# Edge values and queries of a graph layer computed with channels in partitions, then transposed back

## The chip, the cores and the metric

One core of a Trainium2 chip runs the whole kernel. The metric is the device time of one execution in microseconds; the time of a version is the median of its runs. A profiled execution leaves a trace, and all rows quoted here come from it. The engines are called as the profile calls them: PE (TensorE; its weight loads are PEld), DVE (VectorE), ACT (ScalarE), POOL (GpSimd), SP (SyncE, which here only issues DMAs).

## What is computed

A graph attention layer over 6250 nodes and 206250 edges, 64 channels in 4 heads, with a residual and a layer norm. The edge list comes sorted by destination.

```python
Qh = (x @ Wq.T + bq).reshape(n, H, D)
Kh = (x @ Wk.T + bk).reshape(n, H, D)
Vh = (x @ Wv.T + bv).reshape(n, H, D)
Ee = (edge_attr @ We.T + be).reshape(-1, H, D)
score = (Kh[src] * Qh[dst] * (1.0 / np.sqrt(D)) * Ee).sum(-1)
score = jnp.exp(jnp.clip(score, -5.0, 5.0))
msg = Vh[src] * score[..., None]
wV = jax.ops.segment_sum(msg, dst, num_segments=n)
...
x = _layernorm(x + wV.reshape(n, H * D))
```

## The kernel before

**Tiles, groups, steps, rounds.** Edges are cut into 1612 tiles of 128. Eight tiles make a group (202 groups, index g), two groups make a step (s; the last eight groups are steps of their own). Four groups make what is called a round below, and g % 4 (i in the code) is the place in the round: place 0 to place 3. A first stage computes the key and value rows of all nodes into a table in DRAM (`kv_tab`), and the queries of all nodes, split into three bf16 parts, into another. The main loop then runs over g.

**What one group needs.** Keys and values of the source nodes come by indirect DMAs, one a tile, issued by POOL (`gather_kv`, L446) into one of five step buffers; POOL has to wait until the messages of the step that used the buffer are made. Two of the 16 tiles of a step are not gathered but picked: DVE makes one-hot blocks (`hots`, L503), PE multiplies them with the node features (`picks`, L514 and L519, 50 blocks in a round, spread over its four places), ACT copies the result out (`picked`, L526 and L527), PE applies the key and value weights (`picked_kv`, L530 to L535, places 0 and 2), and ACT copies them to the step buffer (`place_kv`, L541, places 1 and 3). The one-hot blocks stand in seven buffers, so a `hots` late in the loop waits for a `picks` two or three pieces back.

**Scores.** `edges` (L560, with the matmuls in L435) multiplies the edge features with the edge weights: the feature block of two tiles (64 channels of each stand in the 128 partitions) is the stationary operand, the block-diagonal weights `we_sb` the moving one of 128 columns. The product stands with edges in partitions and is added onto a bias that ACT has written into that PSUM bank before (`biases`, L564). `queries` (L594) selects the destination's query with a one-hot matrix (`to`, made by ACT in L571 and L577) as the stationary operand of each of the eight tiles. `products` on DVE multiplies the keys with the queries (L600) and the result with the edge values (L601), sums over a head (L604) and clips (L606). `weigh` on ACT is the exponential (L610), `message` on DVE multiplies the values with it (L617).

**Sums.** `onehot_edges` (L585, DVE) and `widen` (L625, ACT) make the one-hot matrix of a step's destinations, `sums` (L630, PE, 16 fp32 matmuls, odd places) adds the messages of its edges, `add` (L644, DVE, even places) adds the sums to a window of node rows. `sums`, `picked_kv`, `place_kv` and `add` use one PSUM bank, `room`.

**Order.** Nothing reorders the work: each engine runs its instructions in the order in which the loop writes them, and waits on semaphores where an operand comes from elsewhere. In iteration g PE runs `picks`, `edges(g+1)`, `sums`, `queries(g+2)`, `picked_kv` (at place 0 the picks come last); ACT the one-hot rows, `widen`, `place_kv`, `biases(g+2)`, `weigh(g)`; DVE `products(g)`, the first `hots`, `add`, `message(g-1)`, `onehot_edges`, the other `hots`. POOL's gathers of the next steps stand behind the message in even iterations. The edge values and the queries have two PSUM banks each.

Of the kernel before, what the change touches and what calls it, by code (L numbers as in the profile page):

```python
# [107 lines left out]
def tile_gnn(ctx: ExitStack, tc: tile.TileContext, x, xT, wT, bias, beT, weT, eT, src, src_rows, dst,  # L108
# [46 lines left out]
    key_rows = consts.tile([NR2, 2, G * P], BF16, name="key_rows")  # L155
# [8 lines left out]
    be_all = consts.tile([P, C], F32, name="be_all")  # L164
# [26 lines left out]
    with tc.tile_pool(name="nodes", bufs=1) as nodes, \  # L191
# [20 lines left out]
        rows_i = nodes.tile([NR2, 2, G * P], I32, name="rows_i")  # L212
        for i in range(NB // CB):
# [15 lines left out]
        nc.sync.dma_start(be_all, beT.to_broadcast([P, C]))  # L229
# [199 lines left out]
    def edge_values(pe, et, n, biased=False):  # L429

        if not biased:
            nc.tensor.matmul(pe[:, :n, :], ones_b, be_p[:, :n, :], start=True, stop=False,
                             skip_group_check=True)
        for u in range(n // 2):
            nc.tensor.matmul(pe[:, 2 * u:2 * u + 2, :], et[:, u, :], we_sb, start=False,  # L435
                             stop=u == n // 2 - 1, skip_group_check=True)
# [20 lines left out]
    with tc.If(rv == 0) as branch:  # L457

        with tc.tile_pool(name="work", bufs=2) as work, \
# [3 lines left out]
            TO, OH, OF, PE, PQ, MSG, KB, SCORE, HOT, FROM, SRC = ({} for _ in range(11))  # L463
# [13 lines left out]
            pe_all = [fixed.tile([P, G, C], F32, name=f"pe{k}") for k in range(2)]  # L477
            pq_all = [fixed.tile([P, G, C], F32, name=f"pq{k}") for k in range(2)]
# [78 lines left out]
            def edges(g):  # L557

                PE[g] = pe_all[g % 2]
                edge_values(PE[g], ET[g], tiles_of(g), g >= 2)  # L560

            def biases(g):
                n = tiles_of(g)
                nc.scalar.activation(pe_all[g % 2][:, :n, :],  # L564
                                     be_all[:, None, :].to_broadcast([P, n, C]), AF.Copy)
# [24 lines left out]
            def queries(g):  # L590
                PQ[g] = pq_all[g % 2]
                n = tiles_of(g)
                for j in range(n):
                    nc.tensor.matmul(PQ[g][:, j, :], TO[g][:, j, :], QW[g], start=j == 0,  # L594
                                     stop=j == n - 1, skip_group_check=True)

            def products(g):
                n = tiles_of(g)
                prod = work.tile([P, G, C], F32, name="prod")
                nc.vector.tensor_mul(prod[:, :n, :], kv_of(g)[:, :n, :C], PQ[g][:, :n, :])  # L600
                nc.vector.tensor_mul(prod[:, :n, :], prod[:, :n, :], PE[g][:, :n, :])  # L601
# [93 lines left out]
            for g in range(4):  # L695
                onehot_rows(g)
                onehot_rows_rest(g)
# [262 lines left out]
```

## Time and profile before

| | |
|---|---|
| median of 3 runs | 2490.64 us (2482.57 to 2494.39) |
| profiled execution | 2496.53 us, of it 2494.6 us between its first and last instruction |
| mean granted TensorE clock | 0.825 |
| PE, DVE, ACT, POOL busy | 78%, 60%, 36%, 54% |
| matmul records, weight-load records | 12299, 12299 |

The profile's page counts an engine as busy while an instruction runs on it; matmul ends are modelled, so that the distance between two starts says more than a duration. An fp32 matmul leaves two records, a bf16 matmul and a transpose one. In a row of the timeline the first number is the start, the second the time until the last of the merged instructions ends, and the bracket tells how long the engine stood idle before and which instruction's signal ended it; "remote" and "issue" mean that no instruction of the trace was found to have ended the wait. POOL runs the gathers one behind the other; an unbroken row of them is called a run below.

### The profile page before, as it was taken

The page shows a single profiled execution, that of the slowest core. Times are in us where ns is not written, and L with a number is a line of the kernel's source. Part 1 is how long each engine was busy: PE and PEld are TensorE (multiplying, and loading weights), DVE is VectorE, ACT ScalarE, POOL GpSimd, SP SyncE. Part 2 cuts the span into 40 slices and gives each one's busy share as a digit, 9 for nine tenths or more (in the row PEclk, how much of TensorE's full clock was granted, in tenths as well). Part 3 has the DMA queues.
Part 4 walks back from the last instruction along what each step waited for, and adds up shares of the span by engine and source line. Part 5 has one row for each costly group of instructions (what it writes and reads, how often), then busy time and mean ns, then how long its engine had stood idle before and what let it go on. Part 6 is the DMA issues. An engine that isn't in the chain of part 4 may idle for free. (4 is left out here: it accounts for less than half of the span.)

```text
span 2494.6 us, 32642 instructions
## 1 busy us (share of the span) xinstructions
PE 1935.9 (78%) x12299; PEld 1331.1 (53%) x12299; DVE 1494.2 (60%) x2314; ACT 908.6 (36%) x1268; POOL 1350.8 (54%) x1434
## 2 busy tenths in 40 slices
PE   4477887887887887877778788788788778788875
PEld 4435555555555555455555555555555555455574
DVE  2356665665666666666556566566666666666653
ACT  1242433433442434233424234233343343342452
POOL 5435555555555555555555555555555555555551
PEclk9978888887887888788788788788888788888865
DMA  4332333333332333333323233233333332332341
GB/s 119 125 96 77 100 91 86 99 97 82 99 97 80 98 91 104 87 83 97 95 82 92 79 101 98 78 99 90 91 103 86 88 101 79 95 93 83 87 114 25
DMA packets 140877, 228.84 MB, mean 92 GB/s; under 512 B 71126, under 2 KB 71576, under 8 KB 140598
## 3 DMA queue, kind: packets, MB, share of 16 engines
q1 hardware_dynamic: 94758, 133.30, 18.3%
q0 software_dynamic: 45568, 92.37, 14.2%
q8 instruction: 98, 1.61, 0.3%
q10 hardware_dynamic: 384, 1.00, 0.2%
q14 instruction: 69, 0.57, 0.1%
HBM read 218.74 MB, written 7.79 MB: 91 GB/s over the span
## 5 line engine op out<-in xcount | busy, mean ns | idle before, releaser
L446 POOL DMA_INDIRECT kv<-kv_tab,src_i x1392 | 1319.3, 948 | 1086.1 <-DVE msg L617 642.3
L503 DVE TENSOR_TENSOR hot<-from,still 128x2048 bf16<-128x2048 bf16 (+1 forms) x611 | 697.2, 1173 | 156.9 <-PE low L519 117.0
L630 PE MATMUL room<-msg,off 128*128 128x64 f32 x3224 | 498.3, 298 | 284.8 <-issue 277.4
L630 PEld LDWEIGHTS room<-msg,off 128*128 128x128 f32 x3224 | 472.9, 220 | 304.3 <-issue 296.0
L514 PE MATMUL pick<-hot,parts 128*128 128x512 bf16 x2350 | 583.8, 401 | 9.3 <-issue 9.0
L541 ACT ACTIVATE kv<-room 128x256 f32<-128x256 f32 x94 | 36.2, 385 | 1379.0 <-PE room L630 511.8
L514 PEld LDWEIGHTS <-parts 128*128 128x128 bf16 x2350 | 235.7, 103 | 299.1 <-issue 88.7
L601 DVE TENSOR_TENSOR prod<-prod,pe 128x512 f32<-128x512 f32 x202 | 138.8, 687 | 418.4 <-remote 323.7
L435 PE MATMUL pe<-we_sb,et 128*128 128x128 f32 x1612 | 292.0, 331 | 110.5 <-ACT pe L564 68.9
L435 PEld LDWEIGHTS pe<-we_sb,et 128*128 128x128 f32 x1612 | 243.3, 229 | 182.7 <-ACT pe L564 88.9
L519 PE MATMUL low<-hot,parts 128*64 128x512 bf16 x2350 | 306.1, 386 | 14.5 <-issue 13.8
L577 ACT ACTIVATE to<-to,one_p 126x1024 bf16<-126x1024 bf16 x202 | 232.0, 1148 | 6.6
L571 ACT ACTIVATE to<-kb,minus_row 126x1024 bf16<-126x1024 bf16 x202 | 230.0, 1139 | 10.9 <-remote 5.5
L519 PEld LDWEIGHTS <-parts 128*64 128x64 bf16 x2350 | 120.3, 110 | 190.0 <-issue 114.8
L625 ACT ACTIVATE off<-of 128x2048 f32<-128x2048 bf16 (+2 forms) x105 | 191.9, 1828 | 52.5 <-remote 20.8
L644 DVE SCALAR_TENSOR_TENSOR acc<-room,above,acc 128x64 f32<-128x64 f32 x103 | 29.0, 282 | 243.2 <-ACT kv L541 177.9
L600 DVE TENSOR_TENSOR prod<-kv,pq 128x512 f32<-128x512 f32 x202 | 137.5, 681 | 25.2 <-remote 6.8
L594 PE MATMUL pq<-qw,to 126*128 126x64 bf16 x1612 | 109.7, 217 | 50.4 <-issue 40.2
L617 DVE TENSOR_TENSOR msg<-kv,score 128x512 f32<-128x512 f32 x202 | 138.7, 687 | 16.9 <-ACT score L610 12.7
L604 DVE TENSOR_REDUCE score<-prod 128x32 f32<-128x512 f32 x202 | 138.3, 685 | 6.9
L594 PEld LDWEIGHTS <-to 126*128 126x128 bf16 x1612 | 103.4, 120 | 61.1 <-issue 56.5
L585 DVE TENSOR_TENSOR of<-still,key 128x2048 bf16<-128x2048 bf16 (+2 forms) x105 | 123.3, 1175 | 0.2
(122 smaller groups left out, 1050.1 us busy)
## 6 DMA issues: line engine op xcount, KB each, us to landing
et<-in_eT SPq DMA_DIRECT2D x100, 512.0 KB
kb<-key_tab SPq DMA_DIRECT2D x201, 252.0 KB
kv<-kv_tab,src_i POOLq DMA_INDIRECT x1392
srcs<-in_src_rows SPq DMA_DIRECT2D x47, 256.0 KB
qw<-q_tab SPq DMA_DIRECT2D x202, 15.8 KB
kv_tab<-kv_sb SPq DMA_DIRECT2D x5, 640.0 KB
q_tab<-q SPq DMA_DIRECT2D x5, 480.0 KB
acc<-in_x SPq DMA_DIRECT2D x48, 32.0 KB
```

The source lines that it names most:

```text
L435: nc.tensor.matmul(pe[:, 2 * u:2 * u + 2, :], et[:, u, :], we_sb, start=False, stop=u == n // 2 - 1, skip_group_check=True)
L446: nc.gpsimd.indirect_dma_start(out=kv_of(g)[:, j, :], out_offset=None, in_=kv_tab[:, :], in_offset=bass.IndirectOffsetOnAxis(ap=src_i[:, t ...
L503: nc.vector.tensor_tensor(HOT[m, c][:, :hi - lo].rearrange("p b (a c) -> p b a c", c=2), pairs(FROM[m])[:, None].to_broadcast(shape), bloc ...
L514: nc.tensor.matmul(hi_mid, parts_flat[:, at:at + 2 * C], hot, start=b == 0, stop=b == NB - 1)
L519: nc.tensor.matmul(low[u * C:(u + 1) * C], parts_flat[:, at:at + C], hot, start=b < 2, stop=b >= NB - 2, skip_group_check=True)
L571: nc.scalar.activation(TO[g][:, :n, :], KB.pop(g)[:, :n * P].rearrange("p (j e) -> p j e", j=n), AF.Square, bias=minus_row3[:3 * W])
L577: nc.scalar.activation(TO[g][:, :n, :], TO[g][:, :n, :], AF.Relu, bias=one_p[:3 * W], scale=-1.0)
L594: nc.tensor.matmul(PQ[g][:, j, :], TO[g][:, j, :], QW[g], start=j == 0, stop=j == n - 1, skip_group_check=True)
L601: nc.vector.tensor_mul(prod[:, :n, :], prod[:, :n, :], PE[g][:, :n, :])
L617: nc.vector.tensor_mul(MSG[s][:, k:k + n, :].rearrange("p g (h d) -> p g h d", h=H), kv_of(g)[:, :n, C:].rearrange("p g (h d) -> p g h d", ...
L625: nc.scalar.activation(OF[s][:, :n, :], OH.pop(s)[:, :n, :], AF.Copy)
L630: nc.tensor.matmul(pa, OF[s][:, j, :], MSG[s][:, j, :], start=j == 0, stop=j == n - 1)
```

## The change

The edge values are computed with the weights as the stationary operand and the edge features of eight tiles as 512 moving columns: one fp32 matmul in place of four of 128 columns, its result with channels in partitions and edges in columns. ACT copies it to SBUF and adds the bias in one instruction, since a channel's bias is now one value a partition (`biased`). The queries are made the same way round: the query window is the stationary operand, the one-hot rows of four tiles the 512 moving columns, two bf16 matmuls in place of eight, the second into the other 64 partitions (`queries`). DVE multiplies the two there (`terms`). PE turns the product back by four transposes of 128 by 128 (`turn`), and `products` is left with one multiplication by the keys. In PSUM `ee` and `qq` are single banks, and the turned product has two.

In the loop `edges` runs three groups ahead, `turn` one, `queries` and `terms` two. PE now runs `edges`, `turn`, `queries` before `sums`; `terms` stands at the end of DVE's iteration, behind all `hots`; ACT runs `weigh` ahead of `widen`, `biased` and `place_kv`. Edge features are fetched one block of two groups earlier. `key_rows` moves to a pool that is freed before the main loop, and `prod` has one buffer.

```diff
-    def edge_values(pe, et, n, biased=False):
-
-        if not biased:
-            nc.tensor.matmul(pe[:, :n, :], ones_b, be_p[:, :n, :], start=True, stop=False,
-                             skip_group_check=True)
...
-            pe_all = [fixed.tile([P, G, C], F32, name=f"pe{k}") for k in range(2)]
-            pq_all = [fixed.tile([P, G, C], F32, name=f"pq{k}") for k in range(2)]
+            ee = fixed.tile([P, G // 2, P], F32, name="ee")
+            qq = fixed.tile([P, G // 2, P], F32, name="qq")
+            qe = [fixed.tile([P, G, C], F32, name=f"qe{k}") for k in range(2)]
...
             def edges(g):
 
-                PE[g] = pe_all[g % 2]
-                edge_values(PE[g], ET[g], tiles_of(g), g >= 2)
-
-            def biases(g):
+                n = tiles_of(g) // 2
+                nc.tensor.matmul(ee[:, :n, :], we_sb, ET[g][:, :n, :], start=True, stop=True)
+
+            def biased(g):
+
+                n = tiles_of(g) // 2
+                EB[g] = work.tile([P, G // 2, P], F32, name="eb")
+                nc.scalar.activation(EB[g][:, :n], ee[:, :n], AF.Identity, bias=be_col)
+
+            def queries(g):
+
                 n = tiles_of(g)
-                nc.scalar.activation(pe_all[g % 2][:, :n, :],
-                                     be_all[:, None, :].to_broadcast([P, n, C]), AF.Copy)
+                for u in range(2):
+                    nc.tensor.matmul(qq[u * C:(u + 1) * C, :n // 2, :], QW[g], TO[g][:, u:n:2, :],
+                                     start=True, stop=True)
+
+            def terms(g):
+
+                n = tiles_of(g) // 2
+                TERM[g] = work.tile([P, G // 2, P], F32, name="term")
+                nc.vector.tensor_mul(TERM[g][:, :n], EB.pop(g)[:, :n], qq[:, :n])
+
+            def turn(g):
+
+                for u in range(tiles_of(g) // 2):
+                    nc.tensor.transpose(qe[g % 2][:, 2 * u:2 * u + 2, :].rearrange("p j c -> p (j c)"),
+                                        TERM[g][:, u, :], ident)
...
-            def queries(g):
-                PQ[g] = pq_all[g % 2]
-                n = tiles_of(g)
-                for j in range(n):
-                    nc.tensor.matmul(PQ[g][:, j, :], TO[g][:, j, :], QW[g], start=j == 0,
-                                     stop=j == n - 1, skip_group_check=True)
-
             def products(g):
                 n = tiles_of(g)
-                prod = work.tile([P, G, C], F32, name="prod")
-                nc.vector.tensor_mul(prod[:, :n, :], kv_of(g)[:, :n, :C], PQ[g][:, :n, :])
-                nc.vector.tensor_mul(prod[:, :n, :], prod[:, :n, :], PE[g][:, :n, :])
+                prod = work.tile([P, G, C], F32, name="prod", bufs=1)
+                nc.vector.tensor_mul(prod[:, :n, :], kv_of(g)[:, :n, :C], qe[g % 2][:, :n, :])
...
-                if g % LG == 0 and g + 2 * LG < NG:
-                    fetch_edges(g // LG + 2)
+                if g % LG == 0 and g + 3 * LG < NG:
+                    fetch_edges(g // LG + 3)
...
-                if 2 <= g + 1 < NG:
-                    edges(g + 1)
+                if g + 3 < NG:
+                    edges(g + 3)
+                if i == 0 and 4 <= g <= 4 * LAST + 2:
+                    picked_kv(0)
+                if g + 1 < NG:
+                    turn(g + 1)
+                if g + 2 < NG:
+                    queries(g + 2)
                 if g - 2 in ends:
                     sums(ends[g - 2])
-                if g + 2 < NG:
-                    queries(g + 2)
-                if i in (0, 2) and 4 <= g <= 4 * LAST + 2:
-                    picked_kv(i // 2)
+                if i == 2 and 4 <= g <= 4 * LAST + 2:
+                    picked_kv(1)
...
                 for mc in ahead[1:]:
                     hots(*mc)
+                if g + 2 < NG:
+                    terms(g + 2)
```

**PE, place 3 of the round of g = 96 to 99.** Before, from the last pick on (`pe` are edge values, `pq` queries; `x4` and `x16` are matmuls of which each leaves two records):

```order
L519 LDWEIGHTS parts
L519 MATMUL low<-hot,parts 64x512
L435 MATMUL pe_883<-we_sb,et 128x128 x4
L630 MATMUL room<-msg,off 128x64 x16
L594 LDWEIGHTS to
L594 MATMUL pq_886<-qw,to 128x64
```

Now, from the same pick on, in the changed kernel's own line numbers (`ee` edge values, `qe` the turned product, `qq` queries, L643 `sums`):

```order
L520 LDWEIGHTS parts
L520 MATMUL low<-hot,parts 64x512
L561 MATMUL ee<-et,we_sb 128x512
L585 MATMUL qe_886<-ident,term 128x128 x4
L573 LDWEIGHTS qw
L573 MATMUL qq<-to,qw 64x512
L573 LDWEIGHTS qw
L573 MATMUL qq<-to,qw 64x512
L643 MATMUL room<-msg,off 128x64 x16
```

The queries have moved from behind the sums to ahead of them, and the four transposes stand there too.

**DVE, from the end of place 3 (g = 99) to the message of place 0 (g = 100).** Before, from the last one-hot block of g = 99:

```order
L503 TENSOR_TENSOR hot<-from,still 128x1024
L600 TENSOR_TENSOR prod<-kv_67,pq_885 128x512
L601 TENSOR_TENSOR prod<-prod,pe_883 128x512
L604 TENSOR_REDUCE score<-prod 128x32
L606 TENSOR_SCALAR score<-score 128x32
L503 TENSOR_TENSOR hot<-from,still 128x2048
L644 SCALAR_TENSOR_TENSOR acc<-room,above,acc 128x64
L644 SCALAR_TENSOR_TENSOR acc<-room,below,acc 128x64
L617 TENSOR_TENSOR msg<-kv_71,score 128x512
```

Now, from the same block (L580 is `terms` of g = 101, L614 the one multiplication left in `products` of g = 100):

```order
L504 TENSOR_TENSOR hot<-from,still 128x1024
L580 TENSOR_TENSOR term<-eb,qq 128x512
L614 TENSOR_TENSOR prod<-kv_67,qe_886 128x512
L617 TENSOR_REDUCE score<-prod 128x32
L619 TENSOR_SCALAR score<-score 128x32
L504 TENSOR_TENSOR hot<-from,still 128x2048
L657 SCALAR_TENSOR_TENSOR acc<-room,above,acc 128x64
L657 SCALAR_TENSOR_TENSOR acc<-room,below,acc 128x64
L630 TENSOR_TENSOR msg<-kv_71,score 128x512
```

As many instructions stand there as before. The first multiplication before needed queries that PE had made an iteration earlier, and the second the edge values of place 3; now the first one needs the queries that PE makes in place 3.

More of the change, by code (lines that the diff above doesn't have):

```diff
@@ L154, in tile_gnn @@
     below = consts.tile([P, 7, 32], F32, name="below")
-    key_rows = consts.tile([NR2, 2, G * P], BF16, name="key_rows")
     n_wide = consts.tile([1, 1], I32, name="n_wide")
@@ L163, in tile_gnn @@
     parts_flat = parts.rearrange("p b i c -> p (b i c)")
-    be_all = consts.tile([P, C], F32, name="be_all")
+    be_col = consts.tile([P, 1], F32, name="be_col")
     acc = consts.tile([P, RING, C], F32, name="acc")
@@ L212, in tile_gnn @@
         rows_i = nodes.tile([NR2, 2, G * P], I32, name="rows_i")
+        key_rows = nodes.tile([NR2, 2, G * P], BF16, name="key_rows")
         for i in range(NB // CB):
@@ L228, in tile_gnn @@
         nc.sync.dma_start(be_sb, beT.to_broadcast([3, C]))
-        nc.sync.dma_start(be_all, beT.to_broadcast([P, C]))
+        for i in range(2):
+            nc.sync.dma_start(be_col[i * C:(i + 1) * C, :], beT.rearrange("o c -> c o"))
         nc.vector.memset(we_sb, 0.0)
@@ L427, in tile_gnn, with edge_values @@
                 rest_of_x()
-    def edge_values(pe, et, n, biased=False):
-        if not biased:
-            nc.tensor.matmul(pe[:, :n, :], ones_b, be_p[:, :n, :], start=True, stop=False,
-                             skip_group_check=True)
+    def edge_values(pe, et, n):
+        nc.tensor.matmul(pe[:, :n, :], ones_b, be_p[:, :n, :], start=True, stop=False,
+                         skip_group_check=True)
         for u in range(n // 2):
@@ L462, in tile_gnn @@
                 tc.tile_pool(name="psum", bufs=1, space=bass.MemoryType.PSUM) as psum:
-            TO, OH, OF, PE, PQ, MSG, KB, SCORE, HOT, FROM, SRC = ({} for _ in range(11))
+            TO, OH, OF, EB, TERM, MSG, KB, SCORE, HOT, FROM, SRC = ({} for _ in range(11))
             still = fixed.tile([P, 4 * P], F32, name="still")
@@ L697, in tile_gnn @@
                 onehot_rows_rest(g)
+            fetch_edges(2)
             for g in range(2):
                 edges(g)
+                biased(g)
                 queries(g)
+                terms(g)
+            turn(0)
+            edges(2)
+            biased(2)
             for mc in pieces(0):
@@ L738, in tile_gnn @@
                     onehot_rows_rest(g + 4)
-                if i == 2 and g < 4 * LAST:
-                    sources(m + 1)
-                if g - 1 in ends:
-                    widen(ends[g - 1])
-                if i in (1, 3) and 4 <= g <= 4 * LAST + 3:
-                    place_kv(m - 1, i // 2)
-                if g + 2 < NG:
-                    biases(g + 2)
                 if now:
@@ L750, in tile_gnn @@
                     add(NS - 2)
+                if g - 1 in ends:
+                    widen(ends[g - 1])
+                if g + 3 < NG:
+                    biased(g + 3)
+                if i == 2 and g < 4 * LAST:
+                    sources(m + 1)
+                if i in (1, 3) and 4 <= g <= 4 * LAST + 3:
+                    place_kv(m - 1, i // 2)
                 if before:
```

## The prediction

> **What bounds the kernel now.** First the busy shares and the list of waits (engine and line that waited, what for, total us, times, longest us).
>
> ```profile
> PE 1935.9 (78%) x12299; PEld 1331.1 (53%) x12299; DVE 1494.2 (60%) x2314; ACT 908.6 (36%) x1268; POOL 1350.8 (54%) x1434
> ...
> POOL kv L446 <- DVE msg L617: 642.3, 139, 27.2
> ...
> DVE prod L601 <- remote: 323.7, 41, 9.5
> ...
> PE room L630 <- issue: 277.4, 385, 1.8
> DVE acc L644 <- ACT kv L541: 177.9, 43, 5.3
> ```
>
> No engine is full. PE stands highest, but part of its time is a stall that no operand explains ("issue", in `sums`), and DVE loses 323.7 us before the second multiplication of `products`, 7.9 us at a time. The timeline of one round shows what ties these together. Rows of PE, DVE, ACT and POOL, in order of time:
>
> ```profile
> 1216.49 0.95 POOL L446 DMA_INDIRECT kv<-kv_tab,src_i  x1 [3.69 <-DVE msg L617]
> ...
> 1222.03 1.16 PE L435 MATMUL pe<-we_sb,et 128*128 128x128 f32 x8
> ...
> 1223.03 1.56 PE L630 MATMUL room<-msg,off 128*128 128x64 f32 x13
> ...
> 1232.75 0.94 POOL L446 DMA_INDIRECT kv<-kv_tab,src_i  x1 [0.30 <-issue]
> ...
> 1236.27 1.33 PE L630 MATMUL room<-msg,off 128*128 128x64 f32 x6 [0.91 <-issue]
> ...
> 1236.32 0.69 DVE L601 TENSOR_TENSOR prod<-prod,pe 128x512 f32<-128x512 f32 x1 [8.26 <-remote]
> 1237.04 0.69 DVE L604 TENSOR_REDUCE score<-prod 128x32 f32<-128x512 f32 x1
> ...
> 1237.64 0.39 ACT L541 ACTIVATE kv<-room 128x256 f32<-128x256 f32 x1 [14.64 <-PE room L630]
> 1237.76 0.18 DVE L606 TENSOR_SCALAR score<-score 128x32 f32<-128x32 f32 x1
> 1237.85 1.21 DVE L503 TENSOR_TENSOR hot<-from,still 128x2048 bf16<-128x2048 bf16 x1
> ...
> 1238.98 0.28 DVE L644 SCALAR_TENSOR_TENSOR acc<-room,above,acc 128x64 f32<-128x64 f32 x1
> ...
> 1239.37 0.68 DVE L617 TENSOR_TENSOR msg<-kv,score 128x512 f32<-128x512 f32 x1
> ...
> 1240.32 0.94 POOL L446 DMA_INDIRECT kv<-kv_tab,src_i  x1 [6.62 <-DVE msg L617]
> ...
> 1248.84 1.22 DVE L503 TENSOR_TENSOR hot<-from,still 128x2048 bf16<-128x2048 bf16 x1 [4.20 <-PE low L519]
> ...
> 1250.93 0.95 POOL L446 DMA_INDIRECT kv<-kv_tab,src_i  x1 [3.41 <-DVE msg L617]
> ...
> 1254.09 3.68 PE L630 MATMUL room<-msg,off 128*128 128x64 f32 x32
> 1254.76 0.69 DVE L601 TENSOR_TENSOR prod<-prod,pe 128x512 f32<-128x512 f32 x1
> 1257.61 0.40 PE L594 MATMUL pq<-qw,to 126*128 126x64 bf16 x8
> ...
> 1262.31 0.39 ACT L541 ACTIVATE kv<-room 128x256 f32<-128x256 f32 x1 [15.79 <-remote]
> ...
> 1262.73 0.28 DVE L644 SCALAR_TENSOR_TENSOR acc<-room,above,acc 128x64 f32<-128x64 f32 x1 [5.22 <-ACT kv L541]
> ...
> 1263.36 0.69 DVE L617 TENSOR_TENSOR msg<-kv,score 128x512 f32<-128x512 f32 x1 [0.16 <-ACT score L610]
> ...
> 1264.32 0.95 POOL L446 DMA_INDIRECT kv<-kv_tab,src_i  x1 [3.69 <-DVE msg L617]
> ```
>
> Look at 1223.2: the edge values that DVE needs in L601 are done there (eight records from 1222.03, each 0.125 us, the next work starting at 1223.03), and DVE gets the signal at 1236.32. In place 1 the sums are done by 1257.8, and ACT, which waits for them, starts at 1262.31. PE's signals are held back while POOL's gathers run: a run of 14 (the last at 1232.75) began at 1216.49 and let go 19.8 us later, a run of 8 began at 1250.93 and let go 11.4 us later, a run of 6 began at 1240.32 and the wait for PE ended 8.5 us later. That is 1.42 us a gather each time. Late in the long hold PE itself slows: 13 matmuls in 1.56 us at 1223.03, then waits without a cause, 385 of them in the trace and 0.72 us each. So a round is three holds and three short answers between them: 19.8, then 4.00 (1236.32 to 1240.32), 8.5, then 2.1 (1248.84 to 1250.93), 11.4, then 2.0 (1262.31 to 1264.32), together 47.8, which is 1264.32 less 1216.49. The holds are counted in gathers, and the change leaves all 28 of them. **What the change can alter are the answers**: what DVE and ACT have to do between a signal's release and the message that frees POOL.
>
> **The change part by part.** The costs of single operations, from the groups by line:
>
> ```profile
> L526 ACT ACTIVATE x<-pick 128x512 f32<-128x512 f32 x47 | 27.6, 587 | 0.0
> ...
> L564 ACT ACTIVATE pe<-be_all 128x512 f32<-128x512 f32 x200 | 117.4, 587 | 12.4 <-DVE prod L601 11.2 <-issue 1.2
> ...
> L600 DVE TENSOR_TENSOR prod<-kv,pq 128x512 f32<-128x512 f32 x202 | 137.5, 681 | 25.2 <-remote 6.8 <-issue 6.4 <-PE room L535 3.9
> ```
>
> *ACT and DVE work.* `biased` copies 128x512 from PSUM, as L526 does in 587 ns; `biases`, which goes, took 587. DVE's two multiplications of 681 and 687 ns become two of the same shape, one operand in PSUM each. Neither engine's total changes.
>
> *PE work, by group.* Edge values: eight fp32 records of 128 columns become two of 512, the same number of columns, 1.0 us either way. Queries: eight records took 0.23 us (1257.61 to the next work at 1257.84); two with 512 columns cost between 0.24 and 0.46 us, from the rows below: twelve `low` matmuls, which alternate between the two halves of the partitions, need 1.41 us, 0.24 a pair, and twelve `pick` ones at most 2.76 us, 0.23 each. I take the pair, since the change also writes the two halves. Transposes: not in the main loop before; four fp32 records of 128 columns are bounded below by L435's 0.125 us each, 0.5 together, and above by four times L386's 424 ns, 1.7 us. I take 0.5, nearer to the distance of the prologue's transposes: four from 111.41 to 112.45, 0.26 each, twice L435's, as it would be at half clock.
>
> ```profile
> 111.41 1.12 PE L386 MATMUL tp<-ident,xs 128*128 128x128 f32 x4
> 112.45 1.11 PE L406 MATMUL ps<-ident,xT_sb 64*128 64x64 f32 x8
> ...
> 1257.84 2.76 PE L514 MATMUL pick<-hot,parts 128*128 128x512 bf16 x12
> ...
> 1237.39 0.63 PE L594 MATMUL pq<-qw,to 126*128 126x64 bf16 x8
> 1238.57 2.07 PE L435 MATMUL pe<-we_sb,et 128*128 128x128 f32 x8 [0.54 <-ACT pe L564]
> ...
> 1251.68 1.49 PE L519 MATMUL low<-hot,parts 128*64 128x512 bf16 x12
> 1253.09 1.16 PE L435 MATMUL pe<-we_sb,et 128*128 128x128 f32 x8
> ```
>
> So PE gains about 0.5 us of work a group and loses instructions: 32 records (weight loads counted) become 16. [...]
>
> *What hides the PE work.* In place 1 the sums end at 1257.8 and are held until 1262.3: 4.5 us of cover for 0.5. In place 3 all of it lies under the long hold. In place 2 PE waits for `place_kv` and for fresh one-hot blocks anyway. In place 0 nothing covers it, and at half clock each step costs nearly double (2.07 us for the edge values at 1238.57, 1.16 at 1222.03): 1.0 for the transposes, less 0.63 for the queries of place 3, which are made before the hold now, less the 0.54 of waiting for `biases`, which goes: -0.2, nothing.
>
> *The answer of place 0.* Before the hold, DVE had done L600, and on release it ran L601, L604, L606, one `hots`, two `add` and the message, 4.00 us to POOL's start. Now it stands at `terms`, one multiplication earlier, behind a signal (queries) that PE gives after 16 records from its last pick (2+2 for the edge values, 4+4 for the transposes, 2+2 for the queries), where the edge values needed 16 before. If the signal is held as that one was, the answer grows by one multiplication, **0.69 us, times the 41 waits: +28 us**. `place_kv` at 1237.64 is no later, and DVE's `add` is the last to be ready.
>
> *The answer of place 2.* The message waits for `weigh`, which now runs ahead of `place_kv`; that wait goes. All of it, by the row of L617:
>
> ```profile
> L617 DVE TENSOR_TENSOR msg<-kv,score 128x512 f32<-128x512 f32 x202 | 138.7, 687 | 16.9 <-ACT score L610 12.7 <-issue 3.5 <-ACT pe L564 0.6
> ```
>
> -13 us. The last eight groups, without picks, gain transposes and lose waits for `biases`: nothing.
>
> *Sum.* +28 - 13 = +15 us on the profiled 2496.5 us. The median of the runs shown is 5.9 us lower: 2490.6 + 15 = **2506 us**.
>
> **The rivals.**
>
> *A, the queries get through.* At place 3 the signal may pass before the hold closes, or early in it: in place 1, L601 ran at 1254.76, 3.8 us into a run of 8. Then DVE does `terms`, the products and one `hots` during the hold, and on release only `place_kv`, `add` and the message remain: add at 1238.0 (end of L541) and not 1238.98, -1.0 us; if the sums are through by then too, ACT starts at 1236.3 and it is -2.3 us. Times 41, less 13 us: 2437 to 2383 us. Against it: as many records stand ahead of the signal as before, in the same place of the run, and 41 of the 47 rounds (x47 in L526) show the wait.
>
> *B, slower: the queries of place 1 are caught.* There `terms` needs a signal that PE gives some 0.7 us after the edge values, 4 us into the run of 8. Edge values at 3.2 us passed; sums at 6.8 were held until 11.4. If the hold closes before 4 us, DVE is stopped ahead of `products` and one `hots`, and the answer of 2.0 us grows by 0.69+0.68+0.69+0.18+1.21 less the 0.42 of waiting for ACT: 3.0 us, times 47: 2506 + 141 = 2647. For it speaks the single signal at 3.2; against it, that queries stand ahead of the 64 records of the sums.
>
> *C, nothing comes of it.* DVE's wait of 4.20 us at 1248.84 is for a pick of PE that ends at about the same time as the hold of 8.5 us. If PE sets it, 0.69 us of DVE ahead of it cost nothing: 2490.6 - 13, or with half of the +28, 2478 to 2492.
>
> *D, slower: PE sets the pace.* Transposes at L386's 424 ns add 1.2 us a group to the 0.5; in place 0, uncovered, 1.2 to 2.4 us times 47: 2562 to 2619. [...] The clock column of the windows shows half clock (0.50) after the hold, in which PE was busy 0.44 of 2 us:
>
> ```profile
> 1226.00:1228.00 2.00, 0.44 (x3) 0.30 (x2) 2.00 (x3) 0.00 (x0) 1.39 (x3) 1.00 0.11 33
> 1238.00:1240.00 2.00, 1.46 (x7) 1.43 (x7) 2.00 (x5) 2.00 (x6) 0.00 (x0) 0.50 0.00 0
> ```
>
> **How the numbers follow.** Forecast 0.42, its own range 2478 to 2533 (from none of the 28 us to all of it with the gain of place 2 absent and 0.3 us more of PE's work showing in place 0, 47 times); A 0.28; C 0.12; B 0.10; D 0.08. A change under 0.5% (2478 to 2503) is about what a measurement here cannot tell from none. The forecast's range has about half in that band and half above; A lies below, C within or a little under it, B and D above. Faster 0.31, same 0.29, slower 0.40. The range leaves out the lower part of A and all of B: 2410 to 2600.
>
> **What would show it.** Right: DVE waits about 8 us for PE at `terms` in some 40 rounds, no longer in `products`; from that release to POOL's next gather 4.7 us; the holds still 1.42 us a gather; L617 no longer waits for ACT; ACT's and DVE's busy time as before; PE's `turn` records 0.125 us apart at full clock. A shows as that wait gone or short and the answer at 2 to 3 us; B as a wait at `terms` in place 1 that ends 11.4 us after the run's start; D as DVE waiting for PE outside the holds. Wrong altogether would be a hold that depends on PE's own records: with 16 fewer a group it would shrink, and the round with it, beyond A.

## The result, and the profile after

The changed kernel takes 2428.11 us (median of 4 runs, 2424.42 to 2431.01) beside 2488.17 us for the kernel before (4 runs): ratio 0.9757, 95% interval 0.9729 to 0.9786. Forecast were 2506 us and an answer that grows; it shrank. The busy shares and waits of the changed kernel, in the columns of the prediction's (its `terms` are L580, `products` L614 to L619, `weigh` L623, `message` L630, `sums` L643, `add` L657, `place_kv` L542, `edges` L561, `biased` L567, `queries` L573, `turn` L585):

```profile
PE 1953.4 (81%) x10687; PEld 1157.5 (48%) x10687; DVE 1479.8 (61%) x2314; ACT 931.0 (38%) x1270; POOL 1352.1 (56%) x1434
...
POOL kv L446 <- DVE msg L630: 584.4, 139, 38.5
...
DVE acc L657 <- ACT kv L542: 336.6, 80, 7.4
...
DVE term L580 <- remote: 183.9, 33, 10.0
...
PE room L643 <- issue: 127.1, 165, 1.9
```

POOL waits 58 us less. DVE's wait for a held signal is still there, at `terms`, but 184 us in place of 324. DVE waits longer in `add` instead, 337 us in place of 178: it is through with its other work earlier and stands there until the release. PE's unexplained stalls in `sums` fell from 277 us to 127. The timeline of the changed kernel, two holds and the answers behind them:

```profile
1223.21 0.94 POOL L446 DMA_INDIRECT kv<-kv_tab,src_i  x1 [3.46 <-DVE msg L630]
...
1234.55 0.38 ACT L542 ACTIVATE kv<-room 128x256 f32<-128x256 f32 x1 [8.43 <-PE low L520]
...
1234.78 0.60 PE L585 MATMUL qe<-ident,term 128*128 128x128 f32 x4
...
1234.96 0.28 DVE L657 SCALAR_TENSOR_TENSOR acc<-room,above,acc 128x64 f32<-128x64 f32 x1 [5.34 <-ACT kv L542]
...
1235.36 0.68 DVE L630 TENSOR_TENSOR msg<-kv,score 128x512 f32<-128x512 f32 x1
...
1236.31 0.94 POOL L446 DMA_INDIRECT kv<-kv_tab,src_i  x1 [3.42 <-DVE msg L630]
...
1242.44 0.41 PE L573 MATMUL qq<-to,qw 126*64 126x512 bf16 x2
...
1242.78 3.99 PE L643 MATMUL room<-msg,off 128*128 128x64 f32 x32
...
1244.10 0.69 ACT L567 ACTIVATE eb<-ee,be_col 128x512 f32<-128x512 f32 x1 [1.51 <-PE room L643]
...
1246.86 0.68 DVE L580 TENSOR_TENSOR term<-eb,qq 128x512 f32<-128x512 f32 x1
...
1247.46 0.68 DVE L614 TENSOR_TENSOR prod<-kv,qe 128x512 f32<-128x512 f32 x1
...
1248.99 1.21 DVE L504 TENSOR_TENSOR hot<-from,still 128x2048 bf16<-128x2048 bf16 x1
...
1252.81 0.94 POOL L446 DMA_INDIRECT kv<-kv_tab,src_i  x1 [0.30 <-issue]
...
1256.33 0.38 ACT L542 ACTIVATE kv<-room 128x256 f32<-128x256 f32 x1 [11.54 <-remote]
...
1256.75 0.28 DVE L657 SCALAR_TENSOR_TENSOR acc<-room,above,acc 128x64 f32<-128x64 f32 x1 [6.55 <-ACT kv L542]
...
1257.14 0.68 DVE L630 TENSOR_TENSOR msg<-kv,score 128x512 f32<-128x512 f32 x1
...
1258.09 0.94 POOL L446 DMA_INDIRECT kv<-kv_tab,src_i  x1 [4.34 <-DVE msg L630]
```

The run of 14 starts at 1236.31 and lets go 20.0 us later, at 1256.33, as before. But `terms` ran at 1246.86, in the middle of it and without any wait (the row has no bracket), and with it the products and a block of comparisons. All 32 matmul records of the sums went through in 3.99 us; before, 13 did, and the rest trickled. So only `place_kv`, `add` and the message are left at the release: 1.8 us to POOL's start, where it was 4.00.

This round is not the usual one: in 38 of 48 runs of 14 DVE does wait at `terms`, by more than 0.5 us. A usual round, and one in which the signal is held to the end:

```profile
868.99 0.94 POOL L446 DMA_INDIRECT kv<-kv_tab,src_i  x1 [3.49 <-DVE msg L630]
...
884.60 0.69 DVE L580 TENSOR_TENSOR term<-eb,qq 128x512 f32<-128x512 f32 x1 [4.98 <-remote]
...
890.82 0.94 POOL L446 DMA_INDIRECT kv<-kv_tab,src_i  x1 [4.39 <-DVE msg L630]
...
2152.25 0.94 POOL L446 DMA_INDIRECT kv<-kv_tab,src_i  x1 [3.58 <-DVE msg L630]
...
2172.10 0.69 DVE L580 TENSOR_TENSOR term<-eb,qq 128x512 f32<-128x512 f32 x1 [10.01 <-remote]
...
2176.71 0.94 POOL L446 DMA_INDIRECT kv<-kv_tab,src_i  x1 [7.29 <-DVE msg L630]
```

A `terms` that starts 15.6 us after the run still leaves time for the products before the release, and the next run comes after 21.8 us, as in the first round. One that starts after 19.9 us does not: the answer is then 4.6 us.

From the starts of POOL's runs in both traces (run of 14 to run of 6 to run of 8 to the next run of 14, mean of the rounds that show the pattern):

| us | before | after |
|---|---|---|
| 14 to 6 | 23.93 (33 rounds) | 22.15 (43) |
| 6 to 8 | 10.39 (43) | 10.32 (43) |
| 8 to 14 | 12.95 (33) | 13.17 (43) |
| first run of 8 in the loop | 213.1 | 221.2 |
| span | 2494.6 | 2422.5 |

A round is 1.6 us shorter, 47 times 77 us; 8 us of it are lost at the start. The step that gained is place 0, from the run of 14 to the run of 6. The step from 8 to 14 gained nothing on the mean.

### The profile page after: what moved, and what is told of

Its sections match the earlier page's. It is cut to its first block, busy times and chain, and to the rows that moved or that the text cites. A ratio compares the mean times of both kernels' runs of the same rounds, so it can differ in the third digit from the quotient of the medians.

```text
span 2422.5 us, 29177 instructions
## 1 busy us (share of the span) xinstructions
PE 1953.4 (81%) x10687; PEld 1157.5 (48%) x10687; DVE 1479.8 (61%) x2314; ACT 931.0 (38%) x1270; POOL 1352.1 (56%) x1434
## 4 chain that ended last, share of the span: by engine, by line
PE 61%; another core or an unknown queue 19%; DVE 8%; ACT 6%; issue 6%; DMA 0%; POOL 0%; DVEq 0%; SPq 0%; ACTq 0%; POOLq 0%
PE pick L515 19%; PE room L643 11%; PE low L520 10%; PE ee L561 7%; PE qe L585 4%; DVE hot L504 3%; PE room L534 3%; PE qq L573 3%; PE room L536 2%; ACT to L598 1%; ACT off L638 1%; ACT eb L567 1%; ACT to L592 1%; PE room L531 1%
## 5 line engine op out<-in xcount | busy, mean ns | idle before, releaser
L643 PE MATMUL room<-msg,off 128*128 128x64 f32 x3224 | 440.6, 288 | 133.5 <-issue 127.1
L643 PEld LDWEIGHTS room<-msg,off 128*128 128x128 f32 x3224 | 412.8, 204 | 161.6 <-issue 153.3
L580 DVE TENSOR_TENSOR term<-eb,qq 128x512 f32<-128x512 f32 x202 | 138.2, 684 | 327.2 <-remote 183.9
L561 PE MATMUL ee<-et,we_sb 128*128 128x512 f32 x404 | 268.6, 736 | 80.3 <-issue 50.4
L542 ACT ACTIVATE kv<-room 128x256 f32<-128x256 f32 x94 | 36.0, 383 | 770.4 <-remote 362.2
L567 ACT ACTIVATE eb<-ee,be_col 128x512 f32<-128x512 f32 x202 | 136.3, 675 | 502.7 <-PE ee L561 224.0
L657 DVE SCALAR_TENSOR_TENSOR acc<-room,above,acc 128x64 f32<-128x64 f32 x103 | 29.2, 283 | 374.0 <-ACT kv L542 336.6
L585 PEld LDWEIGHTS qe<-ident,term 128*128 128x128 f32 x806 | 121.7, 166 | 88.7 <-issue 72.1
L531 PE MATMUL room<-bkv_p,ones_b 3*128 3x256 bf16 x94 | 31.4, 334 | 156.3 <-DVE acc L657 152.1
L585 PE MATMUL qe<-ident,term 128*128 128x128 f32 x806 | 147.6, 315 | 4.5 <-DVE term L580 4.5
L561 PEld LDWEIGHTS ee<-et,we_sb 128*128 128x128 f32 x404 | 71.7, 212 | 154.6 <-issue 114.2
L614 DVE TENSOR_TENSOR prod<-kv,qe 128x512 f32<-128x512 f32 x202 | 137.5, 681 | 3.8 <-issue 0.2
```

What stands on the lines that cost most here:

```text
L561: nc.tensor.matmul(ee[:, :n, :], we_sb, ET[g][:, :n, :], start=True, stop=True)
L567: nc.scalar.activation(EB[g][:, :n], ee[:, :n], AF.Identity, bias=be_col)
L585: nc.tensor.transpose(qe[g % 2][:, 2 * u:2 * u + 2, :].rearrange("p j c -> p (j c)"), TERM[g][:, u, :], ident)
L643: nc.tensor.matmul(pa, OF[s][:, j, :], MSG[s][:, j, :], start=j == 0, stop=j == n - 1)
```

## Experiments

The runs landed on different chips, and these are of two kinds. On some the kernel before takes 2488 to 2546 us, with the holds; here called **held**. On the others it takes 1826 to 1831 us and shows no hold; here called **free**. The comparison above is of the held kind. Each ratio is to the kernel before on the same chip. On a held chip the changed kernel itself was measured only in the comparison above, not beside the runs below.

### The order alone, the form alone

before_order: the kernel before in the new order, as far as it goes.

```diff
-                if g - 2 in ends:
-                    sums(ends[g - 2])
+                if i == 0 and 4 <= g <= 4 * LAST + 2:
+                    picked_kv(0)
                 if g + 2 < NG:
                     queries(g + 2)
-                if i in (0, 2) and 4 <= g <= 4 * LAST + 2:
-                    picked_kv(i // 2)
+                if g - 2 in ends:
+                    sums(ends[g - 2])
+                if i == 2 and 4 <= g <= 4 * LAST + 2:
+                    picked_kv(1)
...
+                if now:
+                    weigh(g)
...
                 if g - 1 in ends:
                     widen(ends[g - 1])
```

> The kernel before with the new order alone where that is possible: queries and the first placing matmuls ahead of the sums, the exponential ahead of the widening and the placing; edge values and queries in their old form. Count: the edge values' signal stands behind as many records as before and the sums behind 16 to 34 more, so the 19.8 us hold catches it, DVE waits 8 us in products, 2470 to 2500 us (place 2 gains at most 17 us). Place: most of the gain of the change is there, 2430 to 2460 us.

split_both: the changed kernel with 24 PE records a group more.

```diff
-                nc.tensor.matmul(ee[:, :n, :], we_sb, ET[g][:, :n, :], start=True, stop=True)
+                for u in range(n):
+                    nc.tensor.matmul(ee[:, u, :], we_sb, ET[g][:, u, :], start=u == 0,
+                                     stop=u == n - 1, skip_group_check=True)
...
-                    nc.tensor.matmul(qq[u * C:(u + 1) * C, :n // 2, :], QW[g], TO[g][:, u:n:2, :],
-                                     start=True, stop=True)
+                    for j in range(n // 2):
+                        nc.tensor.matmul(qq[u * C:(u + 1) * C, j, :], QW[g], TO[g][:, 2 * j + u, :],
+                                         start=j == 0, stop=j == n // 2 - 1, skip_group_check=True)
```

> The changed kernel, but edge values made in four matmuls of 128 columns (not one of 512) and queries in eight of 128 columns (not two of 512): same columns, same order, same results, 24 more PE records a group (weight loads counted). Theory 'count' (how much of PE's work gets its signal out during a run of gathers depends on the number of PE records in it): the signal that the multiplication of the terms waits for falls back to the end of the hold in most rounds, 19.8 us after the run of 14 started, DVE waits some 8 us there, and the time goes back to 2480 to 2510 us. Theory 'place' (it is the order: queries ahead of the sums, and the deeper pipeline): DVE gets its signal at 8 to 12 us as in the changed kernel, and the time stays within 15 us of it, 2425 to 2443.

Both landed on a free chip: before_order 1.0022 (1.0012 to 1.0032), split_both 1.0151 (1.0126 to 1.0175). Without a hold they decide nothing. before_order_2 (1.0028), before_order_3 (1.0036) and split_both_2 (1.0184) are the same kernels, again on free chips; then each met a held chip.

> The same kernel as split_both once more, for a chip on which PE's signals are held. Count: 2465 to 2520 us where the kernel before takes 2490. Place: 2420 to 2445. Where the kernel before takes 1828: 1855 to 1862.

> The same kernel as before_order, for a chip on which PE's signals are held (the kernel before at 2490 to 2550 us). Count alone: ratio to the kernel before 0.99 to 1.03. Order worth most of the gain: 0.97 to 0.985. Where the kernel before takes 1828: 1834.

| held chip | us | kernel before there | ratio, 95% |
|---|---|---|---|
| split_both_3 | 2681.40 | 2546.22 | 1.0542 (1.0506 to 1.0578) |
| before_order_4 | 2627.31 | 2542.51 | 1.0325 (1.0298 to 1.0351) |

Both ratios lie beyond what either theory had written, on the side of 'count'. With the records put back, the new form loses more than the whole gain: it has 40 records a group for edge values, turning and queries, where the kernel before has 32. And the new order with the old form is a loss, not a part of the gain. The timeline of split_both_3 in a run of 14 shows how:

```profile
1205.39 0.94 POOL L446 DMA_INDIRECT kv<-kv_tab,src_i  x1 [3.64 <-DVE msg L633]
...
1213.15 0.30 PE L576 MATMUL qq<-to,qw 126*64 126x128 bf16 x2
...
1215.45 0.30 PE L576 MATMUL qq<-to,qw 126*64 126x128 bf16 x2 [0.49 <-issue]
...
1223.96 0.27 PE L646 MATMUL room<-msg,off 128*128 128x64 f32 x1 [0.94 <-issue]
...
1224.66 0.27 PE L646 MATMUL room<-msg,off 128*128 128x64 f32 x1 [0.44 <-issue]
...
1225.37 4.74 PE L646 MATMUL room<-msg,off 128*128 128x64 f32 x21 [0.44 <-issue]
...
1225.58 0.69 DVE L583 TENSOR_TENSOR term<-eb,qq 128x512 f32<-128x512 f32 x1 [9.54 <-remote]
...
1230.15 0.38 ACT L542 ACTIVATE kv<-room 128x256 f32<-128x256 f32 x1 [4.01 <-PE room L646]
...
1231.91 0.94 POOL L446 DMA_INDIRECT kv<-kv_tab,src_i  x1 [9.07 <-DVE msg L633]
```

PE is already slowed in the queries (L576), and then issues one weight load and one matmul of `sums` per 0.70 us. The signal of the queries comes with the release, 20.2 us into the run, and 21 of the 32 matmuls of `sums` are still to be done behind it. The answer is 6.3 us, 1225.58 to 1231.91. In before_order_4 it is the same with 20 matmuls left, and 6.2 us:

```profile
1225.64 0.94 POOL L446 DMA_INDIRECT kv<-kv_tab,src_i  x1 [3.65 <-DVE msg L617]
...
1245.58 4.53 PE L630 MATMUL room<-msg,off 128*128 128x64 f32 x20 [0.43 <-issue]
1245.74 0.69 DVE L601 TENSOR_TENSOR prod<-prod,pe 128x512 f32<-128x512 f32 x1 [8.54 <-remote]
...
1250.15 0.38 ACT L541 ACTIVATE kv<-room 128x256 f32<-128x256 f32 x1 [17.76 <-PE room L630]
...
1251.91 0.94 POOL L446 DMA_INDIRECT kv<-kv_tab,src_i  x1 [9.10 <-DVE msg L617]
```

Counted over the runs of 14 of all held traces (but the one before the loop has settled): the PE records (weight loads and matmuls) from the start of the run to the last matmul that DVE waits for (`edges` in the old form, `queries` in the new), and when DVE's second multiplication after the start of the run began, in us after that start. It is the one that the quoted rounds show waiting.

| kernel | records, median | start, median | later than 19 us |
|---|---|---|---|
| after | 82 | 14.6 | 6 of 48 |
| picked_late | 93 | 19.7 | 29 of 53 |
| both_late | 93 | 18.8 | 24 of 48 |
| before | 97 | 19.9 | 39 of 44 |
| before_order_4 | 99 | 20.1 | 44 of 46 |
| split_both_3 | 132 | 20.2 | 46 of 47 |

Within the changed kernel alone the rounds differ too. With 69 to 75 records DVE does not wait at all and starts at 9.8 to 10.6 us (8 rounds; so do two with 82, at 9.8 and 11.3). Among the rounds with a wait, the start is at 12.1 us with 72 to 79 records (median of 3), 15.3 with 80 to 87 (18) and 17.0 with 88 to 95 (14). That is some 0.25 us a record, with much scatter (12.1 to 19.9 us within 80 to 87 alone), not far from the 0.35 at which a slowed PE goes on (0.70 a pair, above). So within this kernel the signal comes later, in the median, the more records PE has issued since the run began, up to the end of the hold. Why is not shown, and the count is not all: with 88 to 95 records the new form starts at 17.0 us, but the kernel before at 19.8 (19 rounds). What else holds the old form back stays open.

### The placing matmuls of place 0

picked_late, and both_late, which has the start of start_early (below) as well:

```diff
-                if i == 0 and 4 <= g <= 4 * LAST + 2:
-                    picked_kv(0)
                 if g + 1 < NG:
                     turn(g + 1)
                 if g + 2 < NG:
                     queries(g + 2)
+                if i == 0 and 4 <= g <= 4 * LAST + 2:
+                    picked_kv(0)
```

> The changed kernel with the placing matmuls of place 0 behind the turning and the queries, where the kernel before had them, in place of ahead of them. PE waited 58.8 us there in 46 rounds for the two additions of DVE (1.3 us a round), with the turning and the queries queued behind. Theory 'PE's queue' (where no signal is held, PE sets the pace of the changed kernel, and the kernel before with four transposes added was no slower because its PE does not wait there): POOL's 1348 gathers take 1690 to 1702 us, and not 1717, the time is 1832 to 1842 where the kernel before takes 1828. Rival (PE's own work sets it): 1850 to 1858. Where the kernel before takes about 2490: the turning and the queries of place 0 are made during the hold, the hold stays, 2415 to 2430.

> The same edit together with the start of the run start_early. PE's queue: the start was worth 3.5 us while PE set the pace; with PE's wait gone POOL's gathers set it, and the earlier start counts in full, 4 to 8 us off picked_late: 1824 to 1836 where the kernel before takes 1828. Rival (PE's own work sets it): 1846 to 1855. Where the kernel before takes about 2490: 2405 to 2425.

Both met a held chip (before 2490.23 us): picked_late 2464.30 us, 0.9869 (0.9834 to 0.9905); both_late 2462.29 us, 0.9870 (0.9828 to 0.9912). The expected 2405 to 2430 were missed by 35 us: the order that frees PE from a wait puts more records ahead of the signal (93, not 82), the rounds lose their regular 14, 6, 8, and about half of the gain goes. What they would do on a free chip was not seen.

### The change where nothing is held

> The changed kernel as it is, on the chip that this call gets. The kernel before took 2488 us where it was compared with the change, with PE's signals held during runs of gathers, and 1828 us on the chip of the last four runs, where no wait of DVE is put down to 'remote' and POOL's gathers run almost without a break. Theory 'hold' (the gain of 60 us is a shorter answer to the holds and nothing else): where the kernel before takes about 1828 us, the change gains nothing and the PE work that it adds (4 transposes of 0.125 us each a group, at 202 groups, less what queries and the waits for the biases cost) shows, since PE is busy over 90% of the span: 1835 to 1875 us, slower by 0.5 to 2.5%. Where the kernel before takes about 2488, it is 2428 again. Rival 'shorter path' (the change makes the chain itself shorter, by the form or the order): faster than the kernel before by 1 to 3% in either place.

> The kernel before as it is, for its trace on the chip of this call. Hold: if it takes about 1828 us, no DVE wait on 'remote', POOL starts a gather every 1.25 us across the ends of the runs, PE is busy over 90% and its sums show no waits without a cause; if it takes about 2488, the three holds of 19.8, 8.5 and 11.4 us are there.

Free chip: changed kernel 1856.50 us, ratio 1.0155 (1.0132 to 1.0178); kernel before 1827.70. POOL's groups by line, and its start behind the one long wait, for the kernel before:

```profile
PE 1676.6 (92%) x12299; PEld 1148.1 (63%) x12299; DVE 1490.3 (82%) x2314; ACT 907.5 (50%) x1268; POOL 1363.0 (75%) x1434
...
L446 POOL DMA_INDIRECT kv<-kv_tab,src_i x1392 | 1331.1, 956 | 429.0 <-issue 375.5
...
103.17 0.95 POOL L446 DMA_INDIRECT kv<-kv_tab,src_i  x1 [5.08 <-DVE msg L617]
```

and for the changed kernel:

```profile
PE 1758.8 (95%) x10687; PEld 1054.7 (57%) x10687; DVE 1475.2 (79%) x2314; ACT 938.5 (51%) x1270; POOL 1379.9 (74%) x1434
...
L446 POOL DMA_INDIRECT kv<-kv_tab,src_i x1392 | 1348.4, 969 | 443.0 <-issue 377.7
...
100.06 0.69 DVE L580 TENSOR_TENSOR term<-eb,qq 128x512 f32<-128x512 f32 x1 [17.45 <-ACT eb L567]
...
116.64 0.94 POOL L446 DMA_INDIRECT kv<-kv_tab,src_i  x1 [18.94 <-DVE msg L630]
```

In both POOL runs its gathers without a break from there on, mostly one per 1.25 us, so it sets the length. The 30 us between the two traces are two things. POOL's second start is 13.5 us later (116.64 less 103.17). And its 1348 gathers from there on take 1716.2 us in place of 1699.1, 17 us more. The usual gather is the same, 944 ns (median); but 112 of them take more than 1.0 us, where 57 did before. What stretches these is not shown. Four experiments on the two:

start_early: comparisons, edge values and biased copies ahead of the one-hot rows.

```diff
-            for g in range(4):
-                onehot_rows(g)
-                onehot_rows_rest(g)
             fetch_edges(2)
+            for mc in pieces(0):
+                hots(*mc)
             for g in range(2):
                 edges(g)
                 biased(g)
+                onehot_rows(g)
+                onehot_rows_rest(g)
                 queries(g)
                 terms(g)
...
```

> The changed kernel with its start in another order: the first comparisons ahead of everything else on DVE, edge values and biased copies ahead of the one-hot rows on ACT, rows of groups 2 and 3 last. In the changed kernel POOL stood still for 18.9 us at 97.7 us, until the first message (5.1 us in the kernel before), because DVE waited 17.5 us for the first biased copy, which stood behind eight row operations on ACT, and the comparisons stood behind that on DVE. Theory 'start' (14 of the 30 us by which the change is slower where POOL never stops again are this wait): POOL's second start moves from 116.6 to between 103 and 108 us and the time from 1856 to 1843 to 1848 us. Rival 'pace' (PE's work sets the whole length, and the start only decides where it is waited for): 1853 to 1858. Where the kernel before takes 2490 us: the same 9 to 14 us off 2428.

1853.05 us, 1.0125 (1.0103 to 1.0148): POOL's second start moved by 5 us, from 116.6 to 111.8, and the time by 3.5. That is less than the theory had, and within the rival's 1853 to 1858; most of the start's wait stayed. The 1348 gathers take 1716.2 us as before.

turn_one: one transpose a group, so that three quarters of the turned values are left out.

```diff
-                for u in range(tiles_of(g) // 2):
+                for u in range(tiles_of(g) // 2 if g < 2 else 1):
```

> The changed kernel with one transpose a group in place of four from the third group on, so that three quarters of the turned values are stale: 3 x 0.125 us less of PE's work a group, 76 us in all. Theory 'pace' (PE's added work is why POOL's 1348 gathers after the start take 1717 us in place of 1700, through messages that come late): they fall back to 1700 to 1705 us and the time to 1836 to 1844 us. Rival (the longer path of a group, not PE's work, delays the messages): still 1712 to 1720, 1850 to 1857 us.

1839.22 us, 1.0047 (1.0031 to 1.0063), as 'pace' had it. The 1348 gathers take 1698.5 us, and their mean is back at the kernel before's 956 ns:

```profile
L446 POOL DMA_INDIRECT kv<-kv_tab,src_i x1392 | 1330.5, 956 | 441.7 <-issue 383.3
```

before_turned: four transposes a group in the kernel before, of which nothing uses the result.

```diff
                 PQ[g] = pq_all[g % 2]
                 n = tiles_of(g)
+                for u in range(n // 2):
+                    nc.tensor.transpose(PQ[g][:, 2 * u:2 * u + 2, :].rearrange("p j c -> p (j c)"),
+                                        we_sb, ident)
```

> The kernel before with four transposes of a constant a group ahead of its queries, into the bank that the queries then overwrite: PE's added work alone, 4 x 0.125 us a group, 101 us in all, nothing else moved. Pace: PE is busy 92% of 1826 us already, so POOL's gathers wait for late messages: 1845 to 1890 us. If POOL's gathers alone set the length and PE has room for 100 us, 1826 to 1832 us. Where the kernel before takes 2490 us with held signals: within 20 us of it, since the answers hold none of this work.

1819.57 us, 0.9942 (0.9925 to 0.9958): faster, which neither theory had. Busy times and granted clock (the third number from the right) in the last two of four stretches, kernel before and then before_turned:

```profile
1000.00:1500.00 500.00, 466.46 (x3485) 307.07 (x3484) 418.85 (x618) 249.37 (x331) 379.51 (x396) 0.97 0.44 123
1500.00:1750.00 250.00, 216.72 (x1566) 155.78 (x1564) 177.00 (x271) 120.68 (x159) 189.37 (x199) 0.87 0.43 121
```

```profile
1000.00:1500.00 500.00, 495.70 (x3876) 339.64 (x3876) 435.49 (x641) 258.97 (x345) 378.73 (x399) 1.00 0.45 126
1500.00:1750.00 250.00, 221.31 (x1721) 163.34 (x1718) 180.35 (x276) 125.04 (x164) 189.38 (x200) 0.94 0.44 123
```

PE had more to do, and its granted clock was higher (0.94 and 0.87 in the last stretch). That this is the cause of the shorter time is not shown. It does show that four transposes a group need not cost time on a free chip; in the changed order three of them cost 17 us (turn_one).

gather_less: one gather less a round, in the changed kernel; one tile of edges is left with old keys and values.

```diff
-                        if not is_picked(g, j):
+                        if not is_picked(g, j) and not (g % 4 == 2 and j == 0 and g > 16):
```

> The changed kernel with one gather less a round of four groups (one tile of edges keeps old keys and values), 46 or 47 x 1.25 us of POOL's work, about 58 us. If POOL's gathers set the length: 1856 falls by 50 to 60, to 1796 to 1808 us. If PE sets it: 1840 to 1857 us, and POOL waits for messages instead. Where the kernel before takes 2490 us: one gather less in a run, 1.42 us a round, 67 us off 2428.

1832.54 us, 1.0024 (1.0012 to 1.0035): 24 us less than the changed kernel, between the two answers. POOL then stops for messages (56.9 us, 39 times), so that POOL is near the bound, but not alone; PE, busy for 1601 of the 1630 us from 120 to 1750 there, is the likely other bound; that is a reading.

Two more on free chips:

```diff
+                if g - 2 in ends:
+                    sums(ends[g - 2])
                 if g + 2 < NG:
                     queries(g + 2)
-                if g - 2 in ends:
-                    sums(ends[g - 2])
```

> The changed kernel with the queries behind the sums again, as the kernel before had them. Count and place both put 64 more PE records ahead of the signal that the terms wait for: it comes out at the end of the hold of 19.8 us, the answer of place 0 has the terms, the products and one block of comparisons again, 4.0 us or more in place of 1.8, and the time is 2490 to 2550 us. If the gain came from the place 2 answer or from fewer records elsewhere, the time stays at 2420 to 2445.

queries_late: 2021.52 us, 1.1054 (1.1017 to 1.1090), and 1.1019 as queries_late_2, again free. No hold is needed for that loss: POOL stops 89 times for a message, 220 us. On a held chip this order was not seen.

msg_before_add moves `message(g - 1)` ahead of `add(done)`.

> The changed kernel with the message ahead of the two additions of the closed step on DVE, so that POOL's run of 6 no longer waits for the sums to get through. If the hold is counted in gathers (1.42 us each) and nothing else, the run of 14 and the run of 6 become one of 20, the hold lasts 28.4 us, and the round loses the answer between them, 1.8 us times 47: 2340 to 2360 us. Rival: the longer hold catches the picks and queries of place 0 and 1 as well, DVE and PE wait for each other in it, and the time is 2428 to 2520 us.

1860.23 us, 1.0171 (1.0151 to 1.0192), beside 1.0155 for the changed kernel itself: nothing, as there was no hold to shorten. Whether it gains on a held chip stays open.

## Why the prediction was wrong

**The step that failed** is the answer of place 0: "+0.69 us, times the 41 waits: +28 us", and in it the condition "if the signal is held as that one was". The runs show that `terms` started later than 19 us in 6 of 48 runs of 14, not in 41. In most of the others DVE waited too (38 of 48 runs, 5.0 us in the median), but the signal came early enough for the products to be done before the release. The answer became 1.8 us, not 4.7, and the step from the run of 14 to the run of 6 went from 23.93 to 22.15 us. Where the signal was held to the end, the size was right: 4.6 us, 2172.10 to 2176.71.

The reason given against the rival that came true (A) was that "as many records stand ahead of the signal as before, in the same place of the run". The 16 records behind the last pick were counted rightly. But a count from the start of the run comes out otherwise, 82 against 97 in the median, 71 against 91 in the two quoted rounds. When the run of 1216.49 started in the kernel before, PE still had 9 records of the queries of place 2 to issue and all 18 of the placing matmuls; at 1236.31 in the changed kernel 7 placing records were left. Behind these both have the same 48 records of picks and the same 16. That PE got ahead through the queries' short form, 4 records in place of 16, is the likely reading.

How far the count explains it: 24 records a group put back, with the same columns in the same order, and the signal is at 20.2 us again in 46 of 47 runs, with an answer longer than the one before. So the number of records is a cause. That it is the only one is not shown, since at equal counts the old form is still later (17.0 and 19.8 us, above).

**Rival A** had the step right, and its two cases, 2437 and 2383 us, take in the measured 2428. Its farther case, the sums through as well, was -2.3 us a round; measured are 4.00 to 1.8 us at the quoted place, and 1.8 us for the step from 14 to 6 on the mean. What A did not have is why the signal gets through. **The last sentence of the prediction** named a hold that depends on PE's own records. The length of the hold does not (20.0, 11.3 and 8.5 us, 1.42 a gather, as predicted); what gets through in it does.

**The answer of place 2**, -13 us: right in the mechanism, not in the sum. The message no longer waits for `weigh`, and from the release at 1234.55 to POOL at 1236.31 it is 1.76 us where it was 2.0; times 47 that would be 12 us. But the whole step from 8 to 14 went from 12.95 to 13.17 us on the mean. Its usual length did fall, from 13.4 to 13.2; but in the kernel before 10 of the 33 steps took only 11.9 to 12.0 us, and in the changed one none does. Why these are gone is open.

**ACT's work** was taken as unchanged, since `biased` would take the 587 ns of L526. It takes 675 ns (L567), and ACT's busy time rose from 909 to 931 us.

**PE's added work** was called hidden, 0.5 us a group. The four transposes take 0.60 us (row at 1234.78; the granted clock is 1.00 from 1234 to 1236), so the estimate was nearly right. In place 0, where it had 1.0, they take 1.06 us (from 1259.47; the clock is 0.50 from 1259 to 1261). The mean granted clock did not fall, it rose from 0.825 to 0.858. On a free chip it is not hidden: there turn_one shows 17 us for three of the four. On a held chip no run takes the transposes out, so that it is hidden there is not shown by itself.

**Rivals B, C, D** did not come on the held chip. On the free chips the change is slower by 30 us, of which the transposes are somewhat more than half (17 us, turn_one), a cost to PE of the kind that D named; the rest is the start, a term that the prediction did not have at all. It cost 8 us on the held chip too.

**Left open**: whether the new form with the queries behind the sums would be caught on a held chip (the nearest thing to the forecast); whether the gain there needs the new order at all, beyond that the order without the form loses 3.3%; why the old form is later than the new one at equal counts; and what makes a chip held or free. Every run on record has a granted clock and a span of its own, so none is known in which no records were taken; whether the taking of them has a part in the holds is not shown.

## What to carry to other kernels

Where signals of an engine come late, count what that engine issues from the moment at which the delay begins, not from the last operation in sight: here a few long instructions in place of many short ones (82 records in place of 97 ahead of the signal) went with 60 us less on a held chip, while PE's busy share rose from 78% to 81%. Look at more than one round, too: the round quoted here has no wait at all, and the usual one has 5 us of it. Before a gain is believed, run both kernels on several chips: this change is 2.4% faster on one kind and 1.6% slower on the other, and the bound is another one on each.

## What the runs showed of the hardware

- The same program takes 1826 to 1831 us on some chips and 2488 to 2546 us on others. The gathers themselves are alike (956 and 948 ns each in the kernel before). Of the semaphores that count the ends of DMA transfers, eight record some 2800 steps each on a free chip (before_again, after_again) and 540 to 790 on a held one (before, after). So the two kinds of chip differ in more than PE's signals; why is not shown.
- On a held chip PE slows to a record per 0.35 us late in a run of gathers. Taking as the beginning the first four matmuls in a row with starts 0.6 to 0.8 us apart, 112 to 168 records had been issued in the run of 14 by then (48 runs that show it; medians 127 to 152 in the six held kernels). The free traces before_again, after_again and split_both have no such place.
- Four transposes a group that nothing uses made the kernel before faster by 0.6% on a free chip (before_turned), with a granted clock of 0.964 in place of 0.945.
